# Block places in their own memory, and layer 2's residual, norm and gate as one loop over groups of three tiles

## The chip, the cores and the metric

The kernel runs on one core of a Trainium2 chip. The metric is the device time of one execution in microseconds (us). A core has five engines with an instruction stream each, which run side by side and wait for each other through semaphores: TensorE (PE; its weight loads are listed as PEld), VectorE (DVE), ScalarE (ACT), GpSimd (POOL) and SyncE (SP, which here only issues transfers). Each works through its stream in order. SBUF is the on-chip memory of 128 partitions, PSUM the banks into which TensorE writes, DRAM the memory off the core.

## What is computed

Eight layers run one after the other over 3750 nodes of 256 features and 60000 edges: four graph layers and four feed-forward layers, each added to x.

```python
x = x + L0_gnn(layernorm(x), src, dst, edge_type_8)
x = x + L0_ffn(layernorm(x))
x = x + L1_gnn(layernorm(x), edge_index)
x = x + L1_ffn(layernorm(x))
x = x + L2_gnn(layernorm(x), edge_index)
x = x + L2_ffn(layernorm(x))
x = x + L3_gnn(layernorm(x), edge_index)
x = x + L3_ffn(layernorm(x))
```

Two places matter here. Layer 0's graph part begins with a product of every node's features with the weights of 8 relations and 4 heads:

```python
feat_all = jnp.einsum('ni,rhid->rnhd', inputs, conv_weights)
feat_src_e = feat_all[edge_type, edge_src]
```

Layer 2's graph part is an attention over the incoming edges of a node. Its tail, and the gate with which the feed-forward part after it begins, are:

```python
out = agg.reshape(n, HID) + (x @ Wskip + bskip)
h = jax.nn.gelu(out, approximate=False)
y = x + h
mu = jnp.mean(y, axis=-1, keepdims=True)
var = jnp.var(y, axis=-1, keepdims=True)
return (y - mu) / jnp.sqrt(var + 1e-05) * gamma + beta
...
logits = x @ gate_w + gate_b
```

where the x of the first lines is the normalized input of the layer, and that of the last line the normalized sum after it.

## The kernel before

The 3750 nodes are NT = 30 tiles of P = 128 rows, and x (128 partitions, 30 tiles, D = 256) stays in SBUF through the whole kernel. 

**The head.** `load_edges` packs the edges, two words each, into a table `tab` in DRAM and counts in `falls` where the destinations do not rise. `l0_prepare` (L907) then runs `l0_features` (L861): it loads the weights (`l0_W`) and two attention rows (`l0_at`, one buffer, used twice), takes the statistics of all tiles, and for each tile normalizes (DVE), transposes (PE, L140, into the PSUM tile `xT_ps`), copies to `xT` (ACT, L141), forms the attention products (PE, L147, `lr_ps`, copied out by ACT at L894 and L895, the second into `l0_er`) and then four products 512 wide (`f_ps`, L147, f32). Two of the four are copied by ACT (L903) and two by DVE (L901) into `ft`, which SP stores in the table `l_feat` (L904), 1.04 MB a tile. The pools hold two `ft`, two banks each of `xT_ps` and `lr_ps`, and three of `f_ps`.

Beside this loop stand two chains on small tables, called from `beside()`. `chunks_by_dst` (L514) cuts the edges into chunks by destination: it loads `tab` into `srt` (L522), and writes tables such as `g`, `key_first`, `key_last`, `is_last` to DRAM; it opens and closes its own pools. `block_places` (L347) computes for every edge the place of its entry in a blocked adjacency matrix: it loads the table again as `bp_rec` (125 partitions, 480 edges each, L359), makes 30 counts, two small products in PSUM (`bp_ps`), and the rank loop (L396 to L401) of 30 iterations: a comparison, a scan and a predicated copy, each 125x480. It then stores `put` in `put_dram` (L423), and leaves in `over` whether an edge has found no place. A planner orders the instructions on each engine, so that the chains' instructions stand between the feature loop's. The pools of `block_places` open when those of `chunks_by_dst` are closed, and so lie in the same memory.

`irregular` (L425) adds `over` and `falls`, sums them over the partitions on PE (`falls_ps`, L432) and makes the flag (`irr_flag`, L434). The value is read into registers, and the program branches on it: a general way if it is 1, the regular one if it is 0, which is the case for this data. Nothing of what follows, layer 0's gathers (`gt<-l_feat`, L150) among it, is issued before the branch.

**Layer 2.** `l2_gnn` (L1279) makes q, skip, v and k per tile, stores skip (`sk`, the trace's `l_skip`), and runs the attention, which leaves the sums of each node in `acc` (`l_accu`). Then comes the tail, in three sweeps over the 30 tiles:

- L1338 to L1348: load the skip tile `s` (L1339, 128 KB), product with the reciprocal sum (L1341), add `s` (L1343), Gelu on ACT (L1344), normalize x (L133) and add it (L1347) into `y`, an array of 30 tiles.
- `add_normed` (L983) calls `ln_stats` (L103): statistics of all 30 tiles of y (L110, L111), one Sqrt for all.
- the loop of `add_normed`: normalize y (L133), times gamma (L992), plus beta (L993), added to x (L994), and for each tile `enter` (L1371): statistics of x (L1374, L1375), a Sqrt of one column (ACT, L1377), its reciprocal (L1378), normalize into `en_xn` (L133), store it in the token table `f_x` (L1381), two transposes (PE, L1385), a copy (ACT, L1386), the product with the gate's weights (PE, L147) and the addition of its bias into `f_lg` (DVE, L1389). The pools hold three of each of these.

When all 30 tiles of `f_lg` are there, the gate's softmax and the assignment of tokens to experts follow (L1526 and on), up to the first gather of tokens from `f_x`.

`enter` is also used by layer 3, and `load_row` loads one row and copies it to all partitions.

Of the kernel before, what the change touches and what calls it, by code (L numbers as in the profile page):

```python
# [10 lines left out]
F32 = mybir.dt.float32  # L11
BF16 = mybir.dt.bfloat16
I32 = mybir.dt.int32
# [8 lines left out]
P = 128  # L22
N = 3750
NT = 30
# [34 lines left out]
class Gnn:  # L59
# [287 lines left out]
    def block_places(self, tab):  # L347

        nc = self.nc
        self.put_dram = self.dram.tile([EP, 2, EC], I32, name="put_dram")
        with ExitStack() as st:
            pool, work, pp = self.pools(st, bpl=1, bplw=2, bplp=-1)

            def new(name, dtype=F32, n=EC):
                return pool.tile([EP, n], dtype, name="bp_" + name)
            rec = pool.tile([EP, EC, 2], I32, name="bp_rec")
            nc.sync.dma_start(flat(rec), tab[:E].rearrange("(p c) f -> p (c f)", p=EP))  # L359
            put = pool.tile([EP, 2, EC], I32, name="bp_put")  # L360
            a, b = new("a", I32), new("b", I32)
            T, S = new("T"), new("S")

            nc.vector.tensor_scalar(a, rec[:, :, 1], 7, None, op0=ALU.arith_shift_right)
            nc.vector.tensor_scalar(T, a, float(TD), None, op0=ALU.min)
            nc.vector.tensor_scalar(a, rec[:, :, 0], 10, None, op0=ALU.arith_shift_right)
            nc.vector.tensor_copy(S, a)

            nc.vector.tensor_scalar(a, rec[:, :, 0], 3, None, op0=ALU.arith_shift_right)
            nc.vector.tensor_scalar(a, a, 127, None, op0=ALU.bitwise_and)  # L370
            nc.vector.scalar_tensor_tensor(put[:, 1, :], rec[:, :, 1], 256.0, a, op0=ALU.mult, op1=ALU.add)
            same = new("same")
            nc.vector.memset(same[:, 0:1], 1.0)
            nc.vector.tensor_tensor(same[:, 1:], T[:, 1:], T[:, :EC - 1], ALU.is_equal)


            end = new("end")
            nc.vector.tensor_scalar(end, T, T[:, EC - 1:], None, op0=ALU.is_equal)
            nc.vector.scalar_tensor_tensor(end, S, 1.0, end, op0=ALU.add, op1=ALU.mult)
            cnt = new("cnt", n=NT)  # L380
            for t in range(NT):
                junk = work.tile([EP, EC], F32, name="bp_eq")
                nc.vector.tensor_scalar(junk, end, float(t + 1), None, op0=ALU.is_equal, op1=ALU.add,
                                        accum_out=cnt[:, t:t + 1])
            diag = new("diag", n=EP)
            nc.vector.tensor_scalar(diag, self.ident[:EP, :EP], T[:, 0:1], None, op0=ALU.mult)
            ps = pp.tile([EP, EP + NT], F32, name="bp_ps")
            nc.tensor.matmul(ps[:, :EP], self.ones[:EP, :EP], diag, start=True, stop=True)
            nc.vector.tensor_scalar(diag, ps[:, :EP], T[:, EC - 1:], None, op0=ALU.is_equal)
            nc.vector.tensor_tensor(diag, diag, self.before[:EP, :EP], ALU.mult)  # L390
            nc.tensor.matmul(ps[:, EP:], diag, cnt, start=True, stop=True)
            carry = new("carry", n=NT)
            nc.vector.tensor_copy(carry, ps[:, EP:])
            rank = new("rank")
            nc.vector.memset(rank, 0.0)
            for t in range(NT):  # L396
                eq = work.tile([EP, EC], F32, name="bp_eq")
                run = work.tile([EP, EC], F32, name="bp_run")
                nc.vector.tensor_scalar(eq, S, float(t), None, op0=ALU.is_equal)
                nc.vector.tensor_tensor_scan(run, same, eq, carry[:, t:t + 1], ALU.mult, ALU.add)  # L400
                nc.vector.copy_predicated(rank, eq.bitcast(I32), run)  # L401
            nc.vector.tensor_scalar(rank, rank, -1.0, None, op0=ALU.add)

            lim = end
            nc.vector.tensor_scalar(lim, T, 1.0, 256.0, op0=ALU.is_lt, op1=ALU.mult)
            small = new("small")
            nc.vector.tensor_scalar(small, T, 4.0, 128.0, op0=ALU.is_lt, op1=ALU.mult)
            nc.vector.scalar_tensor_tensor(lim, small, 128.0, lim, op0=ALU.add, op1=ALU.add)
            nc.vector.tensor_scalar(small, T, float(TD), 128.0 * (JS - 1), op0=ALU.is_ge, op1=ALU.mult)
            nc.vector.tensor_tensor(lim, lim, small, ALU.add)  # L410
            nc.vector.tensor_tensor(lim, rank, lim, ALU.is_ge)
            nc.vector.tensor_reduce(carry[:, 0:1], lim, AX.X, ALU.add)
            nc.vector.tensor_tensor(self.over, self.over, carry[:, 0:1], ALU.add)

            for t, before in ((1, T), (1, small), (1, small), (2, small), (3, small), (4, small)):
                nc.vector.scalar_tensor_tensor(small, T, float(t), before, op0=ALU.is_ge, op1=ALU.add)
            nc.vector.tensor_copy(a, rank)
            nc.vector.tensor_scalar(b, a, 7, None, op0=ALU.arith_shift_right)
            nc.vector.tensor_scalar(a, a, 127, None, op0=ALU.bitwise_and)
            nc.vector.tensor_tensor(small, small, b, ALU.add)  # L420
            nc.vector.scalar_tensor_tensor(small, small, float(NT), S, op0=ALU.mult, op1=ALU.add)
            nc.vector.scalar_tensor_tensor(put[:, 0, :], a, float(NCB), small, op0=ALU.mult, op1=ALU.add)
            nc.sync.dma_start(self.put_dram, put)  # L423
# [437 lines left out]
    def l0_features(self, tab, er, beside):  # L861
# [5 lines left out]
        with ExitStack() as st:  # L867
# [18 lines left out]
            for t in range(NT):  # L886
# [3 lines left out]
                self.transposed(xT, xn, pp)  # L890
                ft = xp.tile([P, R, D + H], F32, name="ft")
                ps = pp.tile([P, 2 * RH], F32, name="lr_ps")
# [14 lines left out]
    def l0_prepare(self, tab):  # L907

        nc, R, H = self.nc, 8, 4
        self.feat = self.dram.tile([NP * R, D + H], F32, name="l0_feat")  # L910
        self.er_dram = self.dram.tile([P, NT * R * H], F32, name="l0_er_dram")
        with ExitStack() as st:
            pool, = self.pools(st, l0er=1)
            er = pool.tile([P, NT, R * H], F32, name="l0_er")
            def beside():
                self.over = self.edges.tile([EP, 1], F32, name="over")
                self.chunks_by_dst(tab, CAPS)
                self.block_places(tab)
            self.l0_features(self.feat, er, beside)
            nc.sync.dma_start(self.er_dram, flat(er))  # L920
# [358 lines left out]
    def l2_gnn(self, entry):  # L1279
# [4 lines left out]
        with ExitStack() as outer:  # L1284
# [46 lines left out]
            with ExitStack() as st:  # L1331
                wp, ap = self.pools(st, l2fin=3, l2y=1)
# [3 lines left out]
                y = ap.tile([P, NT, D], F32, name="l2_y")  # L1336
                for t in range(NT):
                    s = wp.tile([P, D], F32, name="s")  # L1338
                    nc.sync.dma_start(s, sk[t * P:(t + 1) * P])  # L1339
                    a = wp.tile([P, H, DH], F32, name="a")  # L1340
                    nc.vector.tensor_tensor(a, acc[:, t, :D].rearrange("p (h d) -> p h d", h=H),  # L1341
                                            rd[:, t, :].unsqueeze(2).to_broadcast([P, H, DH]), ALU.mult)
                    nc.vector.tensor_tensor(flat(a), flat(a), s, ALU.add)  # L1343
                    nc.scalar.activation(flat(a), flat(a), AF.Gelu)  # L1344
                    xn = wp.tile([P, D], F32, name="xn")
                    self.normed(xn, self.x, stats, t)
                    nc.vector.tensor_tensor(y[:, t, :], xn, flat(a), ALU.add)  # L1347
                wp, pp = self.pools(st, l2en=3, l2enp=-3)  # L1348
                self.add_normed(ap, y, "L2_gnn_gamma", "L2_gnn_beta", "l2n",
                                lambda t: self.enter(entry, t, wp, pp))  # L1350
# [20 lines left out]
    def enter(self, e, t, wp, pp):  # L1371
        nc = self.nc
        st = wp.tile([P, 6], F32, name="en_st")
        nc.vector.bn_stats(st, self.x[:, t, :])  # L1374
        nc.vector.bn_aggr(e["mv"][:, t, :], st)  # L1375
        r = e["rstd"][:, t:t + 1]
        nc.scalar.activation(r, e["mv"][:, t, 1:2], AF.Sqrt, bias=self.eps, scale=1.0)  # L1377
        nc.vector.reciprocal(r, r)  # L1378
        xn = wp.tile([P, D], F32, name="en_xn")
        self.normed(xn, self.x, e["stats"], t)  # L1380
        nc.sync.dma_start(e["tab"][t * P:(t + 1) * P], xn)  # L1381
        xT = wp.tile([P, 2, P], F32, name="en_xT")
        bank = pp.tile([P, 3, P], F32, name="en_ps")
        for c in range(2):
            nc.tensor.transpose(bank[:, c, :], xn[:, c * P:(c + 1) * P], self.ident)  # L1385
        nc.scalar.copy(xT, bank[:, :2, :])  # L1386
# [924 lines left out]
```

## Time and profile before

Three runs took 5733.62, 5743.11 and 5742.64 us, the median 5742.64. The profile is of one execution of its own:

| | |
|---|---|
| profiled execution | 6525.78 us |
| its span, first to last instruction | 6524.0 us |
| mean granted TensorE clock | 0.798 |
| longer than the median of the runs by | 783 us (13.6%) |
| first gather of layer 0 | at 370.0 us |
| layer 2's tail, L1334 to the last f_lg | 3946.7 to 4116.9 us |
| first gather of layer 2's tokens | at 4165.2 us |

Times within the kernel are those of this execution. The page has the span in 40 equal slices; a digit is the busy share of a slice in tenths, and PEclk is the clock granted to TensorE in tenths of full speed:

```profile
PE   6826655596476665975555553798879898896885
DVE  5634433794233346435565557403532342266435
POOL 0046666676566658864444440012025444452124
PEclk9957777798677777987777775698589999998896
```

A slice is 163 us. The first two are the head: POOL has nothing to do in them. Slices 24 and 25 (the count starts at 0) hold layer 2's tail and the start of the feed-forward part: VectorE falls from 7 to 4, and the granted clock is 0.5 and 0.6.

### The profile page before, as it was taken

Reading aid. Unit: us, or ns where it says so; the run is one execution under the profiler, and the core shown is the slowest. Engines: PE = TensorE matmul, PEld = TensorE weight load, DVE = VectorE, ACT = ScalarE, POOL = GpSimd, SP = SyncE. Lnnn points to the kernel's source line nnn. Section 1 sums busy time; section 2 is a strip of 40 time slices with the busy share of each in tenths; the row PEclk is TensorE's granted clock in tenths of the full one; section 3 lists DMA queues with packets and bytes.
Section 4 is the critical chain, followed back from the end, with each engine's and each line's share of the span. In section 5 each row is a group of like instructions: output and inputs, shape, how many; then the busy total and the mean of one; then the engine's idle time right before and its main releaser. Section 6 shows DMA issues by size and latency. Waiting matters only on the chain. (4 is left out here: it accounts for less than half of the span.)

```text
span 6524.0 us, 64749 instructions
## 1 busy us (share of the span) xinstructions
PE 4544.5 (70%) x20324; PEld 3306.5 (51%) x20438; DVE 3068.4 (47%) x7333; ACT 2064.1 (32%) x4862; POOL 2921.8 (45%) x2845
## 2 busy tenths in 40 slices
PE   6826655596476665975555553798879898896885
PEld 2425554465455553634444442576545565564673
DVE  5634433794233346435565557403532342266435
ACT  1125544312455552324343442222531121110121
POOL 0046666676566658864444440012025444452124
PEclk9957777798677777987777775698589999998896
DMA  4334444202344431145555551222434554455113
GB/s 147 132 95 115 115 116 112 43 2 72 99 119 117 115 79 35 22 130 160 159 159 157 147 148 45 90 91 74 162 124 139 137 134 128 132 145 162 50 56 114
DMA packets 431195, 714.02 MB, mean 109 GB/s; under 512 B 117474, under 2 KB 308645, under 8 KB 426748
## 3 DMA queue, kind: packets, MB, share of 16 engines
q0 software_dynamic: 145168, 379.81, 23.0%
q1 hardware_dynamic: 267064, 316.47, 15.5%
q10 hardware_dynamic: 18612, 13.50, 0.7%
q8 instruction: 166, 2.72, 0.2%
q14 instruction: 185, 1.52, 0.1%
HBM read 583.81 MB, written 125.15 MB: 109 GB/s over the span
## 5 line engine op out<-in xcount | busy, mean ns | idle before, releaser
L1965 PE MATMUL sum_ps<-gt,oh 128*128 128x260 f32 (+2 forms) x3150 | 1018.8, 485 | 368.2 <-issue 155.4
L1965 PEld LDWEIGHTS sum_ps<-gt,oh 128*128 128x128 f32 x3150 | 749.4, 244 | 565.0 <-issue 187.7
L150 POOL DMA_INDIRECT gt<-l_vk,srci x525 | 497.6, 948 | 549.1 <-issue 179.4
L156 POOL DMA_INDIRECT blocks<-put x480 | 648.2, 1350 | 155.0 <-issue 145.6
L150 POOL DMA_INDIRECT gt<-l_h,srci x525 | 496.6, 946 | 333.8 <-issue 228.8
L150 POOL DMA_INDIRECT gt<-l_feat,g x525 | 501.7, 956 | 317.2 <-issue 235.2
L1947 DVE TENSOR_TENSOR gt<-gt,bank 128x1792 f32<-128x1792 f32 x225 | 453.5, 2016 | 123.6 <-remote 52.8
L1839 ACT ACTIVATE oh<-iota,dloc 128x128 f32<-128x128 f32 x1575 | 481.4, 386 | 19.1 <-PE sum_ps L1965 15.7
L150 POOL DMA_INDIRECT gt<-l_mtab,l_idxm x300 | 296.3, 988 | 359.9 <-ACT gt L2170 184.3
L150 POOL DMA_INDIRECT gt<-l_xtab,srci x262 | 253.2, 966 | 396.7 <-DMA l_xtab<-xt 192.4
L2184 PE MATMUL two_ps<-l_twox,slab 128*128 128x512 bf16 x1026 | 354.8, 391 | 28.1 <-issue 27.8
L147 PE MATMUL y_ps<-f_w,hT 128*128 128x256 f32 x1600 | 359.4, 384 | 15.5 <-DVE y L1075 13.5
L2184 PEld LDWEIGHTS <-slab 128*128 128x128 bf16 x2160 | 213.5, 99 | 268.2 <-issue 40.9
L2184 PE MATMUL two_ps<-l_twom,slab 128*128 128x512 bf16 x1020 | 341.9, 379 | 0.0
L147 PEld LDWEIGHTS y_ps<-f_w,hT 128*128 128x128 f32 x1600 | 306.8, 193 | 67.2 <-DVE y L1075 18.0
L2186 PE MATMUL third_ps<-l_thirdx,slab 128*128 128x257 bf16 x1080 | 300.7, 280 | 31.5 <-issue 17.6
L2186 PE MATMUL third_ps<-gt,oh 128*128 128x257 f32 x1124 | 275.4, 389 | 37.1 <-DVE oh L2173 28.5
L2186 PE MATMUL third_ps<-l_thirdm,slab 128*128 128x257 bf16 x1080 | 294.8, 273 | 3.2
L1830 ACT ACTIVATE ohT<-rows,iota_p 128x896 f32<-128x896 bf16 x225 | 235.2, 1045 | 142.8 <-DMA rows<-dl_dram 69.7
L1322 PE MATMUL q_ps<-l_qt,ohT 128*128 128x256 f32 x1050 | 250.1, 391 | 31.4 <-DVE gt L1328 18.7
L1976 PE MATMUL bank<-less,at_row 112*128 112x8 f32 (+1 forms) x146 | 41.7, 358 | 317.2 <-issue 156.9
L1922 ACT ACTIVATE fw<-fw 112x128 f32<-112x128 f32 x76 | 23.5, 309 | 754.5 <-DVE fw L1921 608.9
(544 smaller groups left out, 8807.8 us busy)
## 6 DMA issues: line engine op xcount, KB each, us to landing
rows<-dl_dram SPq DMA_DIRECT2D x225, 224.0 KB
slab<-adT SPq DMA_DIRECT2D x36, 960.0 KB
slab<-ad SPq DMA_DIRECT2D x30, 1152.0 KB
l_feat<-ft SPq DMA_DIRECT2D x30, 1040.0 KB
f_w<-in_L_ffn_w_dram SPq DMA_DIRECT2D x18, 1024.0 KB
adT<-db_rowT SPq DMA_DIRECT2D x36, 480.0 KB
ad<-db_row SPq DMA_DIRECT2D x36, 480.0 KB
f_yt<-y SPq DMA_DIRECT2D x114, 128.0 KB
```

The source lines that it names most:

```text
L147: self.nc.tensor.matmul(ps, xT[:, c, :], w[:, c, :], start=(c == 0), stop=(c == kc - 1))
L150: return self.nc.gpsimd.indirect_dma_start(out=out, out_offset=None, in_=table, in_offset=bass.IndirectOffsetOnAxis(ap=idx, axis=0))
L156: inst = self.nc.gpsimd.indirect_dma_start(out=table, out_offset=bass.IndirectOffsetOnAxis(ap=idx, axis=0), in_=src, in_offset=None)
L1322: nc.tensor.matmul(ps[:, j, :], ohT[:, j * P:(j + 1) * P], flat(q[:, ds(tiles[j], 1), :]), start=True, stop=True)
L1830: nc.scalar.activation(t, rows, AF.Abs, bias=self.iota_p, scale=-1.0)
L1839: nc.scalar.activation(oh[:, j, :], self.iota, AF.Abs, bias=self.dloc[:, c + j:c + j + 1], scale=-1.0)
L1922: nc.scalar.activation(fw, fw, AF.Exp)
L1947: nc.vector.tensor_tensor(rows, rows, wj.unsqueeze(3).to_broadcast([P, GC, H, DH]), ALU.mult)
L1965: nc.tensor.matmul(open_[1], oh[:, j, :], gt[:, j, :W], start=starts(k), stop=starts(k + 1))
L1976: nc.tensor.matmul(f_ps, at, less, start=True, stop=True)
L2184: nc.tensor.matmul(flat(ps), block, flat(two[n][:, blocks[i][1]]), start=(i == 0), stop=(i == len(blocks) - 1))
L2186: nc.tensor.matmul(ps3[:, :D + 1], block, rhs, start=(i == 0), stop=(i == len(all3) - 1))
```

## The change

In the head, `beside()` opens the pools of `block_places` before it calls `chunks_by_dst`, and hands them over, so that they no longer share memory with the chunk tables. The pool of `bp_ps`, a PSUM bank, is thereby open through both chains. The feature loop puts its transposed tile and its attention products in one tile `l0_bank` of one bank in place of two (`xT_ps` and `lr_ps`). The body of `block_places` is unindented and otherwise unchanged.

In layer 2, the tail becomes one loop over groups of T = 3 tiles in four stages: `arm` of group k, `norm` of group k-1, `join` of group k, `enter_rows` of group k-1. The skip load is one transfer of three tiles, the additions of skip, of the gated row and of beta are 768 wide, the Gelu too. The normalized x is made on ACT, as Identity with a scale and a bias. Gamma is a factor of the same operation that subtracts the mean, and the reciprocal deviation is applied with the addition to x, to which beta has been added before. The Sqrt takes three columns. The array y of 30 tiles is gone; its groups live in a pool with two buffers, as do the tiles of `enter_rows`, which had three.

```diff
-    def block_places(self, tab):
+    def block_places(self, tab, pool, work, pp):
...
-        with ExitStack() as st:
-            pool, work, pp = self.pools(st, bpl=1, bplw=2, bplp=-1)
...
-                self.transposed(xT, xn, pp)
+                bank = pp.tile([P, 2 * P + 2 * RH], F32, name="l0_bank")
+                turned, ps = bank[:, :2 * P].rearrange("p (c n) -> p c n", c=2), bank[:, 2 * P:]
+                for c in range(2):
+                    nc.tensor.transpose(turned[:, c, :], xn[:, c * P:(c + 1) * P], self.ident)
+                nc.scalar.copy(xT, turned)
                 ft = xp.tile([P, R, D + H], F32, name="ft")
-                ps = pp.tile([P, 2 * RH], F32, name="lr_ps")
                 self.product(ps, xT, wl)
...
-                self.chunks_by_dst(tab, CAPS)
-                self.block_places(tab)
+                with ExitStack() as st2:
+
+                    pools = self.pools(st2, bpl=1, bplw=2, bplp=-1)
+                    self.chunks_by_dst(tab, CAPS)
+                    self.block_places(tab, *pools)
...
-                wp, ap = self.pools(st, l2fin=3, l2y=1)
+                T = 3
+                ap, wp, pp = self.pools(st, l2y=1, l2fin=2, l2enp=-3)
                 rd = ap.tile([P, NT, H], F32, name="l2_rd")
                 nc.vector.tensor_scalar(rd, acc[:, :NT, D:], TINY, None, op0=ALU.max)
                 nc.vector.reciprocal(rd, rd)
-                y = ap.tile([P, NT, D], F32, name="l2_y")
-                for t in range(NT):
-                    s = wp.tile([P, D], F32, name="s")
-                    nc.sync.dma_start(s, sk[t * P:(t + 1) * P])
-                    a = wp.tile([P, H, DH], F32, name="a")
-                    nc.vector.tensor_tensor(a, acc[:, t, :D].rearrange("p (h d) -> p h d", h=H),
-                                            rd[:, t, :].unsqueeze(2).to_broadcast([P, H, DH]), ALU.mult)
-                    nc.vector.tensor_tensor(flat(a), flat(a), s, ALU.add)
-                    nc.scalar.activation(flat(a), flat(a), AF.Gelu)
-                    xn = wp.tile([P, D], F32, name="xn")
-                    self.normed(xn, self.x, stats, t)
-                    nc.vector.tensor_tensor(y[:, t, :], xn, flat(a), ALU.add)
-                wp, pp = self.pools(st, l2en=3, l2enp=-3)
-                self.add_normed(ap, y, "L2_gnn_gamma", "L2_gnn_beta", "l2n",
-                                lambda t: self.enter(entry, t, wp, pp))
+                gamma = self.load_row(ap, ins["L2_gnn_gamma"], "l2n_g")
+                beta = self.load_row(ap, ins["L2_gnn_beta"], "l2n_b")
+                mv, rstd = stats
+                off = ap.tile([P, NT], F32, name="l2_off")
+                nc.vector.scalar_tensor_tensor(off, mv[:, :, 0], -1.0, rstd, op0=ALU.mult, op1=ALU.mult)
+                ymv, yr = ap.tile([P, NT, 2], F32, name="l2_ymv"), ap.tile([P, NT], F32, name="l2_yr")
+                ys, arms = {}, {}
+                def arm(t0):
+                    s = wp.tile([P, T, D], F32, name="s")
+                    nc.sync.dma_start(s, sk[t0 * P:(t0 + T) * P].rearrange("(t p) d -> p t d", p=P))
+                    a = wp.tile([P, T, D], F32, name="a")
+                    for t in range(T):
+                        nc.vector.tensor_tensor(a[:, t].rearrange("p (h d) -> p h d", h=H),
+                                                acc[:, t0 + t, :D].rearrange("p (h d) -> p h d", h=H),
+                                                rd[:, t0 + t, :].unsqueeze(2).to_broadcast([P, H, DH]), ALU.mult)
+                    nc.vector.tensor_tensor(a, a, s, ALU.add)
+                    nc.scalar.activation(flat(a), flat(a), AF.Gelu)
+                    y = wp.tile([P, T, D], F32, name="y")
+                    for t in range(t0, t0 + T):
+                        nc.scalar.activation(y[:, t - t0], self.x[:, t], AF.Identity, bias=off[:, t:t + 1],
+                                             scale=rstd[:, t:t + 1])
+                    arms[t0], ys[t0] = a, y
+                def join(t0):
+                    y, x = ys[t0], self.x[:, t0:t0 + T]
+                    nc.vector.tensor_tensor(y, y, arms.pop(t0), ALU.add)
+                    for t in range(T):
+                        bn = wp.tile([P, 6], F32, name="bn")
+                        nc.vector.bn_stats(bn, y[:, t])
+                        nc.vector.bn_aggr(ymv[:, t0 + t], bn)
+                    nc.scalar.activation(yr[:, t0:t0 + T], ymv[:, t0:t0 + T, 1], AF.Sqrt, bias=self.eps, scale=1.0)
+                    nc.vector.tensor_tensor(x, x, beta.unsqueeze(1).to_broadcast([P, T, D]), ALU.add)
+                def norm(t0):
+                    y = ys.pop(t0)
+                    nc.vector.reciprocal(yr[:, t0:t0 + T], yr[:, t0:t0 + T])
+                    for t in range(t0, t0 + T):
+                        row, x = y[:, t - t0], self.x[:, t]
+                        nc.vector.scalar_tensor_tensor(row, row, ymv[:, t, 0:1], gamma, op0=ALU.subtract, op1=ALU.mult)
+                        nc.vector.scalar_tensor_tensor(x, row, yr[:, t:t + 1], x, op0=ALU.mult, op1=ALU.add)
+                    self.enter_stats(entry, t0, t0 + T, wp)
+                for t0 in range(0, NT + T, T):
+                    if t0 < NT:
+                        arm(t0)
+                    if t0:
+                        norm(t0 - T)
+                    if t0 < NT:
+                        join(t0)
+                    if t0:
+                        self.enter_rows(entry, t0 - T, t0, wp, pp)
```

`enter` is split in two. `enter_stats` holds the statistics of tiles t0 to t1 and one Sqrt over their columns; `enter_rows` holds one reciprocal over them, and for each tile the rest of `enter` unchanged: the normalized row `en_xn`, its store in `f_x`, the transposes, the copy, the product with the gate's weights and the bias. `enter` itself calls both for one tile.

## The prediction

> **What bounds the kernel now.** The page's busy row first: no engine is full, so what the change is worth must be read in its two stages.
>
> ```profile
> PE 4544.5 (70%) x20324; PEld 3306.5 (51%) x20438; DVE 3068.4 (47%) x7333; ACT 2064.1 (32%) x4862; POOL 2921.8 (45%) x2845
> ```
>
> The head next, in the timeline around the branch (start us, duration us, engine, line, operation; in brackets the idle time before and what ended it):
>
> ```profile
> 310.31 3.70 PE L147 MATMUL f_ps<-l_W,xT 128*128 128x512 f32 x8 [0.90 <-DVE ft L901]
> 318.79 0.67 DVE L901 COPY ft<-f_ps 128x512 f32<-128x512 f32 x1
> 324.11 0.72 DVE L399 TENSOR_SCALAR bp_eq<-bp_S 125x480 f32<-125x480 f32 x2
> 328.26 0.72 DVE L399 TENSOR_SCALAR bp_eq<-bp_S 125x480 f32<-125x480 f32 x2
> 350.73 0.19 PE L432 MATMUL falls_ps<-ones,over 125*1 125x1 f32 x2 [36.72 <-DVE over L430]
> 351.22 0.14 DVE L434 TENSOR_SCALAR irr_flag<-falls_ps 1x1 int32<-1x1 f32 x1
> 370.01 5.34 POOL L150 DMA_INDIRECT gt<-l_feat,g  x1 [14.23 <-DMA seg_b<-seg]
> ```
>
> TensorE ends layer 0's products at 314.0 and stands still until 350.73: VectorE works alone on the place chain, two rank iterations per 4.15 us. Only then is the flag there, on which the branch and the first gather hang. The chain is late because it starts late. In SyncE's waits (engine, line, who ended the wait: us in total, times, longest) its load stands behind the last release of the chunk tables; the tile view has that load issued at 232.6, while the table it reads was loaded once already at 46.2:
>
> ```profile
> SPq L359 <- DMA is_last_dram<-is_last: 5.6, 1, 5.6
> ```
>
> Layer 2's tail runs from 3946.66 (reciprocal) to 4116.9 (last f_lg), 170.3 us. The window rows give length, then busy us of PE, PEld, DVE, ACT, POOL with counts, the PE clock, the DMA share and GB/s; the group rows give busy us, mean ns, and the idle time before:
>
> ```profile
> 3946.50:4117.00 170.50, 50.25 (x181) 36.57 (x182) 129.62 (x466) 35.29 (x95) 0.16 (x1) 0.51 0.15 46
> 3946.50:3987.60 41.10, 0.00 (x0) 0.00 (x0) 40.67 (x118) 13.41 (x31) 0.00 (x0) 0.56 0.30 87
> L1389 DVE TENSOR_TENSOR f_lg<-en_ps,f_gb 128x8 f32<-128x8 f32 x30 | 5.0, 167 | 40.4 <-PE en_ps L147 40.4
> L1386 ACT COPY en_xT<-en_ps 128x256 f32<-128x256 f32 x30 | 11.2, 372 | 69.0 <-PE en_ps L1385 69.0
> ```
>
> VectorE sets the pace: full for 41 us, then idle 30 times for about 1.35 us (40.4 in all), each time until TensorE has one tile's gate product. TensorE, ScalarE and the transfers have room.
>
> **Part A, the head.** Removed: the wait at L359. In the changed program's order the load stands right behind the chunks' own load of that table, at about 34 us, and the chain's VectorE work lies among the 60 feature copies (L901), the last of it with 23 copies to come. No instruction is saved, so the gain is what the chain hides behind. TensorE's own pace is 15.63 us per two tiles (lr_ps at 163.03 to 178.66), 3.9 us per VectorE copy. I add the chain's rows, start to start, between the copies: a count .57, a rank iteration 2.08 ((328.26−324.11)/2), a copy .60.
> - Copies 5 to 12 carry the front of the chain: 38.4 us of VectorE from 79.19, so copy 12 at 117.6 (before 120.4).
> - Copies 13 to 19 at TensorE's pace: about 145 (before 146.7).
> - Copies 20 to 36 carry the rank loop, 80.2 us of VectorE where TensorE needs 17×3.9 = 66.3: about 225 (before 214).
> - 23 more at 3.9: about 315; the flag at 315.5 to 316 instead of 351.36. **Gain 36 us.**
>
> Before, TensorE lost 9 us here in another place:
>
> ```profile
> 114.18 1.12 PE L147 MATMUL lr_ps<-l_wlr,xT 128*128 128x64 f32 x4 [8.97 <-ACT xT L141]
> ```
>
> There a copy queued on ScalarE behind a DMA issue that waited for key_first (10.5 us). In the new order those issues (L666) stand behind the xT copies of two more tiles, so I expect 1 to 2 us of it; ScalarE's later copies and the issues queue behind it. If it stays and none of VectorE's excess (about 26 us) finds slack, the gain is 20. The upper end, 45, takes the excess as hidden.
>
> The moved load passes the second l_at load on SyncE, which is not issued before 46.2 for want of a buffer: nothing. Merging xT_ps and lr_ps in one bank makes a transpose wait for the er copy two tiles back instead of the xT copy, under 2 us after it in 7.8 us per tile: nothing. Late next are the 12 feature stores still on SyncE behind the places' store: the last, 1.04 MB at the 128 GB/s of this loop, lands 8 us after its copy, near 326; the first gather stays 18.65 us behind the flag, near 334. Were that cover gone it would cost the difference, a few us.
>
> **Part B, layer 2.** VectorE's 30 passes for the normalized input go to ScalarE, the 30 gamma products into the subtraction, the residual into the scaling; skip, gate and beta additions become 768 wide, and 31 Sqrt become 20. Rows start to start: a 256-wide operation .335 us, bn with aggregation .39, xn .325, f_lg and a reciprocal .08. A 768-wide addition is not in this stage: three times .335 is the upper end (1.0), 480 wide takes .58 and 640 wide .74, whose slope of 1.07 ns an element gives .88; I take .88. The fused operation with two inputs exists in layer 1 (L1275, L1276, 479 ns busy where a plain one shows 415), so .335 to .40; I take .335 and leave .06×60 = 4 us to the range.
>
> Per group of three: products 1.0, three wide additions (+s, +a, +beta) 2.64, six fused 2.0, six bn 2.34, xn .98, f_lg .24, reciprocals .16: 9.36 us. Ten groups 93.6, less 1.8 for two beta additions pulled into the attention's end, plus the reciprocal 1.95, plus the adjacency set-up that falls here before and after (8.4): 102.2 us, against 129.6 busy.
>
> Idle: following one period in the new order, VectorE waits about .94 us at the pair of f_lg and .64 at the third, where before it waited 1.35 per tile; 1.6 a group, nine groups 14.4 (ends 0 and 3.5 a group: 0 and 31). Tail 2 us. End 3946.7+102.2+14.4+2 = 4065: 52 us earlier, less 2 to 4 for what was pulled into the attention: **gain 48 us**, range 25 to 66. Skip loads of 393 KB go out five deep ahead, then among the f_x stores on SyncE, two groups early (22 us) at a DMA share of 0.15: hidden. ScalarE holds Gelu .9, three Identity 1.2, two Sqrt .6, three copies 1.1 and two table loads 2.6 (the other kinds' means from the stage's ACT rows, Gelu scaled up from .42 for 256, an estimate), 6.5 of 11 us. What follows hangs on f_lg (the first token gather is issued at 4165), so the whole gain passes on.
>
> **A rule against this.** Gelu and Sqrt now alternate, and each change reloads ScalarE's table: 18 loads where there were 2.
>
> ```profile
> 3987.80 0.42 ACT L1344 ACTIVATE a<-a 128x256 f32<-128x256 f32 x1 [0.91 <-DVE a L1343]
> 3988.23 1.28 ACT L112 ACT_TABLE_LOAD   x1
> ```
>
> By the row a load is 1.28 us and begins .01 after the Gelu, ahead of the Sqrt's wait; 16 more cost 20.5 us of ScalarE's 135 idle. The Trainium skill ("ScalarE: Activation LUTs", section "What ACT_TABLE_LOAD costs") adds a drain of about 1380 ns, 2.66 us a switch. The row shows none ahead of the load; what comes behind it no row of this stage shows, as ScalarE then waits for data. By the rule Gelu ends 1.4 us later, the third tile's copy waits for it, the period goes from 10.95 to 12.3 and the stage gains 36. I take the row and keep 36 in the range.
>
> **Sum.** 36+48 = 84 us of the profiled 6525.78: about 6442. The median of the plain runs is 12% shorter, so the gain lies between .88 and 1 of that; as both stages run on TensorE and VectorE without gathers, I take .95: 80 us, **5662**.
>
> **Rivals.** (1) The head becomes VectorE-bound, excess and stall staying: 20+48 = 68, 5678. For it, the rank loop needs 4.7 us a copy against 3.9; against it, the 7 copies between and slack in the six f_ps and ft buffers. Chance .15. (2) Layer 2 keeps its latencies, with drains or 3.5 to 4.5 us idle a group: 27 there, 36+27 = 63, 5683; with both short 45, 5700. For it, each f_lg waits for a chain over three engines (xn, transposes, copy, product: 2.3 to 2.6 us); against it, two tiles' chains now overlap. Chance .15, both .05. (3) Slower: the loop is serialised over ScalarE's table loads. The two stages each wait for a Gelu and a Sqrt with their loads (2.2+1.9) and two full entry chains (5) on top of 9.36: 18.5 us a period, 21.3 with drains, where it decides from 19.4 (1.95+8.4+2+10×19.4 eats the head's 36 too): at 21.3 it is 225 us, 55 longer, and with the head's 36 about 19 longer, 5761. Against it, the loads run ahead of the waits, and other stages' work stands between. Chance .04. (4) The last feature store holds the first gather anyway: it lands near 326 at most, so a few us; inside the forecast. That the places don't move is excluded by the new order.
>
> **Numbers.** The forecast .61, rivals (1) .15, (2) .15, both .05, (3) .04. The likeliest alone spans 5640 to 5680 (profiled gains 65 to 105 by the ends above); the range runs to the case of both short and some run-to-run spread (the runs of before span 9.5 us): 5632 to 5705. A difference under 0.2% (11.5 us) can't be told from none: faster .93, same .03 (the far end of both short), slower .04.
>
> **What would show it.** Flag near 316, places' load near 34, first gather near 334; TensorE's longest gap before the flag under 3 us. Layer 2's tail about 118 us, period near 11, VectorE's wait for the gate product 14 us in all, 18 loads with a Gelu or Sqrt starting right behind one. Wrong if the last product is past 330, if the gather moves less than the flag, or if periods exceed 13 us.

## The result, and the profile after

The changed kernel takes 5672.25 us (median of 4 runs, 5671.77 to 5673.43) beside 5742.51 before (4 runs): a ratio of 0.9882, 95% interval 0.9864 to 0.9899, 70 us less. The forecast was 5662 with a range of 5632 to 5705.

Its profiled execution spans 5671.6 us. The profile of before, 6524.0 us, fits a slower chip: on the chip of three of the experiments below the kernel before has a median of 6508.8 us. Which chip the profile came from is not on record. A second profile of the kernel before, on a chip where it takes 5748 us, spans 5752.2 and is used from here on for sums over the whole kernel. The head and layer 2's tail last the same in both (flag at 351.2 and 350.2, tail 170.2 us in each), so the lines shown with the prediction can be set beside the new ones.

The page of the changed kernel, busy row and VectorE's and TensorE's 40 slices of 142 us:

```profile
PE 4457.1 (79%) x20438; PEld 3256.8 (57%) x20438; DVE 3041.6 (54%) x7203; ACT 2097.9 (37%) x4877; POOL 2923.4 (52%) x2845
PE   5957777687677746988887748987799999994996
DVE  7624544895334366448888883026533433566336
```

VectorE's first slice is at 7 where it was 5, in both profiles of before: the chain has moved forward. The head's timeline, as before with start and length in us, engine, line and operation:

```profile
316.07 0.69 DVE L902 COPY ft<-f_ps 128x512 f32<-128x512 f32 x1 [3.24 <-PE f_ps L147]
319.35 0.19 PE L430 MATMUL falls_ps<-ones,over 125*1 125x1 f32 x2
319.45 0.69 DVE L902 COPY ft<-f_ps 128x512 f32<-128x512 f32 x1 [2.69 <-PE f_ps L147]
320.06 0.13 DVE L432 TENSOR_SCALAR irr_flag<-falls_ps 1x1 int32<-1x1 f32 x1
337.39 5.35 POOL L150 DMA_INDIRECT gt<-l_feat,g  x1 [9.23 <-DMA ends_b<-ends_dram]
```

TensorE's gap of 36.7 us before the flag's product is gone; VectorE now waits for TensorE at the end. The flag comes at 320.06 (before 351.22), the first gather at 337.39 (370.01). Layer 2's tail in its window row (length, then busy us of PE, PEld, DVE, ACT and POOL):

```profile
3277.50:3402.25 124.75, 46.56 (x180) 36.97 (x181) 106.48 (x331) 60.83 (x102) 0.15 (x1) 0.52 0.19 60
```

and VectorE's main wait in it (us in all, times, longest):

```profile
DVE f_lg L1440 <- PE en_ps L147: 18.1, 28, 1.3
```

The tail takes 124.75 us instead of 170. VectorE is busy 23 us less and waits 22 us less for the gate product (40.4 before).

From the second profile of before to the changed kernel's (5752.2 to 5671.6) the 80.6 us sum up so. The first gather comes 31.4 us earlier. From it to the start of the tail it is 5.3 less; two other profiles with the old head, the merged bank's and the changed tail's, are 8.3 and 6.5 us shorter there than the second profile of before, so this is put down to scatter. From the start of the tail to the first token gather it is 42.1 less (218.5 to 176.4), and the rest is 1.8.

### The profile page after: what moved, and what is told of

The parts are those of the page before. It is cut to its first block, busy times and chain, and to the rows that moved or that the text cites. A ratio compares the mean times of both kernels' runs of the same rounds, so it can differ in the third digit from the quotient of the medians.

```text
span 5671.6 us, 64613 instructions
## 1 busy us (share of the span) xinstructions
PE 4457.1 (79%) x20438; PEld 3256.8 (57%) x20438; DVE 3041.6 (54%) x7203; ACT 2097.9 (37%) x4877; POOL 2923.4 (52%) x2845
## 4 chain that ended last, share of the span: by engine, by line
PE 45%; DVE 16%; POOL 12%; DMA 9%; issue 8%; ACT 4%; DVEq 0%; SPq 0%; ACTq 0%; another core or an unknown queue 0%; POOLq 0%
POOL gt L150 11%; PE sum_ps L2016 7%; PE third_ps L2237 7%; PE two_ps L2235 5%; PE y_ps L147 5%; PE hT_ps L1824 3%; PE y_ps L1833 2%; PE h_ps L1617 2%; PE db_psT L2149 2%; PE q_ps L1326 2%; DMA gt<-l_h,srci 2%; DMA gt<-l_vk,srci 2%; PE qkvs_ps L147 2%; PE h_ps L1260 2%; DMA gt<-l_feat,g 2%
## 5 line engine op out<-in xcount | busy, mean ns | idle before, releaser
L2016 PE MATMUL sum_ps<-gt,oh 128*128 128x260 f32 (+2 forms) x3150 | 996.7, 482 | 272.3 <-ACT gt L1999 171.0
L2235 PE MATMUL two_ps<-l_twom,slab 128*128 128x512 bf16 x1080 | 359.8, 379 | 0.0
L2149 PE MATMUL db_psT<-db_oh,db_oh 128*128 128x128 bf16 x690 | 187.7, 409 | 66.9 <-ACT db_rowT L2150 32.4
L1892 ACT ACTIVATE oh<-oh,ones 128x896 f32<-128x896 f32 x225 | 234.4, 1042 | 7.3
```

The costliest lines, as they stand in the source:

```text
L1892: nc.scalar.activation(flat(oh), flat(oh), AF.Relu, bias=self.ones[:, 0:1], scale=-1.0)
L2016: nc.tensor.matmul(open_[1], oh[:, j, :], gt[:, j, :W], start=starts(k), stop=starts(k + 1))
L2149: nc.tensor.matmul(ps[:, j, :], lhsT, rhs, start=(i == 0), stop=(i == len(some) - 1))
L2235: nc.tensor.matmul(flat(ps), block, flat(two[n][:, blocks[i][1]]), start=(i == 0), stop=(i == len(blocks) - 1))
```

## The experiments

Experiments 1 to 4, 5 to 8, 9 to 11 and 12 each ran on a chip of their own, together with the kernel before.

**1. A second profile of the kernel before**

> The kernel before, unchanged, for a second profile. The first profiled execution took 6525.78 us, 783 us more than the median of the plain runs. If that execution was a single odd one, this profile spans about 5740 us, with the flag of the head near 351 us, the first gather near 370 us and layer 2's tail again about 170 us long. If the profiler always slows this kernel so, the span is again near 6520 us, and the durations in the head and in the tail can't be set beside those of the changed kernel without a scale.

5754.0 us beside 5747.7: the head and the tail as in the first profile. The 783 us lay neither in these stages nor with the profiler. The two profiles differ in the stages between: from the first gather of layer 0 to its reciprocal it is 855 us in the first and 696 here.

**2 and 3. The two halves alone.** The diffs are the two parts of the change.

> Only the head changed (pools of the block places opened early, one bank for transposed tile and attention products); layer 2's tail as before. By the traces the first gather came 32.6 us earlier (370.0 to 337.4). If everything behind the gather just shifts, this gains 30 to 33 us: about 5710. If a part is given back behind the branch (the gathers of layer 0 then start while stores are still landing), the gain is under 27 us: over 5715.

> Only layer 2's tail changed; head as before. By the traces the tail is 44.5 us shorter (170.3 to 125.8). If all of it passes on to the token gather and nothing of it depends on the head, the gain is 42 to 45 us: about 5699, and with the head's alone the two sum to the whole change (70 us). If the attention before it pays for the y passes that were pulled into its end, the gain is 38 us or less.

The head alone takes 5716.19 us (ratio 0.9946, 0.9933 to 0.9960), 31.5 less; the tail alone 5702.95 (0.9927, 0.9914 to 0.9941), 44.8 less. The sum, 76, is that of the whole change on another chip of the same kind (5752.41 to 5676.14) and, within the intervals, of the first result. The head's gain passes through undiminished, and the attention doesn't pay for the pulled-in passes beyond what these intervals show.

**4. The merged bank alone**

```diff
-                self.transposed(xT, xn, pp)
-                ps = pp.tile([P, 2 * RH], F32, name="lr_ps")
+                bank = pp.tile([P, 2 * P + 2 * RH], F32, name="l0_bank")
+                turned, ps = bank[:, :2 * P].rearrange("p (c n) -> p c n", c=2), bank[:, 2 * P:]
```

> The kernel before with only the merge of transposed tile and attention products in one PSUM bank; places and tail as before. Prediction's step: it costs nothing, within 2 us of before (5740 to 5745). Rival: a tile's transpose now waits for the second copy out of the shared bank and TensorE loses up to 0.5 us in each of 30 tiles, hidden until the end of the products behind the place chain here, so that the time is the same but TensorE's last product of the head comes up to 15 us later than 314.0.

Ratio 1.0002 (0.9994 to 1.0010), and TensorE's last product ends at 313.9 (314.0 and 313.0 in the two profiles of before): it costs nothing, and hides nothing.

**5 to 8, the changed kernel again and three edits of it**

> The changed kernel itself, on the chip of the next three, as what they are set beside: about 0.988 of before, flag of the head near 320, layer 2's tail near 125 us.

5676.14 us, ratio 0.9869 (0.9853 to 0.9886).

*One load of the table.*

```diff
-        rec = pool.tile([EP, EC, 2], I32, name="bp_rec")
-        nc.sync.dma_start(flat(rec), tab[:E].rearrange("(p c) f -> p (c f)", p=EP))
...
+                    rec = pools[0].tile([EP, EC, 2], I32, name="srt")
+                    self.nc.sync.dma_start(flat(rec), tab[:E].rearrange("(p c) f -> p (c f)", p=EP))
-                    self.chunks_by_dst(tab, CAPS)
-                    self.block_places(tab, *pools)
+                    self.chunks_by_dst(tab, CAPS, rec)
+                    self.block_places(rec, *pools)
```

> The changed kernel, but the block places use the table copy that the chunks have loaded (one tile for both), so the second load of 480 KB at 33.6 us is gone. In the changed kernel VectorE's product L879 waited 4.75 us for a weight load that ended 1.02 us of waiting before, and every later step of the head stands 3.1 us later. Theory: the second table load takes its bandwidth among the weight loads, so that product starts near 43.9 instead of 47.0, the flag comes 2 to 4 us earlier (316 to 318), the time is 2 to 4 us below the changed kernel's. Rival: the weights' lateness has another cause (the order of the loads), the product starts at 47 again and nothing is gained.

The product among the weights, first in the changed kernel's second run, then here, in VectorE's timeline:

```profile
46.78 2.29 DVE L879 TENSOR_TENSOR l_pr<-l_W,l_at 128x2048 f32<-128x2048 f32 x1 [4.87 <-DMA l_W<-_L_gnn_conv_weights_dram]
```

```profile
44.11 2.29 DVE L878 TENSOR_TENSOR l_pr<-l_W,l_at 128x2048 f32<-128x2048 f32 x1 [0.22 <-DVE l_st L110]
```

The wait for a weight load is gone. The first feature copy is at 59.85 (62.52 in the changed kernel on this chip; 59.64 and 58.64 before), the last at 316.57 against 318.59, so 2.0 us of the 2.7 reach the end of the head. The time, 5672.89, is 3 us lower, which fits but is within the intervals; the trace carries the theory.

*Key loads issued by GpSimd.*

```diff
-                    eng = (nc.sync, nc.scalar)[(i // B + c) % 2]
+                    eng = (nc.sync, nc.gpsimd)[(i // B + c) % 2]
```

> The changed kernel, but those half of the key loads (endk) that ScalarE issued are issued by GpSimd; the order on TensorE and VectorE is the same. In the changed kernel ScalarE waits 9.8 us for key_first at 121.5 and TensorE then 4.9 us for its copies. Theory: that wait goes, TensorE's 4.9 us with it, and the flag comes 4 to 5 us earlier (315 to 316). Rival: VectorE bounds this stretch by the chain's work before and behind it, and the flag moves under 1.5 us; or GpSimd issues the small loads so slowly that VectorE waits for the ends, and the flag comes later than 320.

The first run of the changed kernel, its ScalarE and then its TensorE, at that place:

```profile
122.12 0.18 ACT L895 COPY ft<-l_bank 128x32 f32<-128x32 f32 x1 [9.79 <-DMA endk<-key_first]
```

```profile
126.20 3.78 PE L147 MATMUL f_ps<-l_W,xT 128*128 128x512 f32 x4 [4.88 <-ACT ft L904]
```

A copy is ready to go and waits behind an issue that waits for its data; TensorE then waits for the buffer that the copy would free. With the issues on GpSimd:

```profile
123.32 3.65 PE L147 MATMUL f_ps<-l_W,xT 128*128 128x512 f32 x8
128.18 3.27 PE L147 MATMUL f_ps<-l_W,xT 128*128 128x512 f32 x7 [1.21 <-DVE ft L902]
```

The last copy comes at 313.91 in place of 318.59, the flag at 314.52, the gather at 332.16. The time is 5673.35 us, again within the intervals. The instruction order on TensorE and VectorE in the head is the changed kernel's own.

*No change of table.*

```diff
-                    nc.scalar.activation(flat(a), flat(a), AF.Gelu)
+                    nc.scalar.activation(flat(a), flat(a), AF.Identity)
```

> The changed kernel with layer 2's gated row as Identity in place of Gelu (this leaves out layer 2's Gelu), which needs no other table than the Sqrt: the 17 or so loads between Gelu and Sqrt in the tail go, everything else stays. Theory (the switch costs 1.28 us and lies in ScalarE's idle time): period 11.4 to 11.7 us as in the changed kernel (11.63) and the tail within 3 us of 124.8. Rival (loads and what follows them are on the path): period 10.5 or less, tail under 115 us.

The time is 5678.59 us. The 17 loads are gone, ScalarE's busy time in the tail falls from 60.8 to 39.3 us, and the tail is 128.9 us, 4 longer: the planner, which counts the loads, put the rows elsewhere, and VectorE waits 23.5 us for the gate product. VectorE's busy time is nearly the same (105.0). So taking the loads away did not shorten the tail, which speaks against the rival; what the identical order would take without them was not shown.

**9 to 11, on the slower chip (before: 6508.8 us)**

*The normalized input on VectorE again.*

```diff
-                        nc.scalar.activation(y[:, t - t0], self.x[:, t], AF.Identity, bias=off[:, t:t + 1],
-                                             scale=rstd[:, t:t + 1])
+                        nc.vector.tensor_scalar(y[:, t - t0], self.x[:, t], mv[:, t, 0:1], rstd[:, t:t + 1],
+                                                op0=ALU.subtract, op1=ALU.mult)
```

> The changed kernel with one part of the tail undone: the normalized input made by VectorE again (30 operations of .335 us from start to start) and not by ScalarE. Theory (VectorE's own work sets the period, the rest is waits for the gate product): period about 12.6 us against 11.63, tail about 133 to 135 us against 124.8. Rival (the chain over TensorE and ScalarE sets it and VectorE's work fills idle time): tail under 128 us.

Window row of the tail, then VectorE's wait:

```profile
3900.40:4034.90 134.50, 46.53 (x180) 36.93 (x181) 114.28 (x355) 48.40 (x78) 0.16 (x1) 0.52 0.18 56
DVE f_lg L1440 <- PE en_ps L147: 20.1, 30, 1.3
```

The tail takes 134.5 us with a period of 12.67 (f_lg at 3957.50, 3970.17); VectorE is busy 7.8 us more and waits 2.0 more. Its work sets the period, as the theory says. The time is 6455.74 us, ratio 0.9920 (0.9901 to 0.9939).

*Groups of 5* (`T = 5`).

> The changed kernel with groups of 5 tiles in layer 2's tail (6 groups in place of 10, 12 table loads fewer or so). In the changed kernel VectorE waits 1.70 us in a period of three tiles. Theory (one pair and the last tile of a group wait, whatever its size): about 2 to 2.5 us idle in a period of five tiles, 11 us in all against 18.1, VectorE's work the same or 2 us less, more filling at the start; tail 118 to 123 us. Rival (each gate product waits in its turn, idle goes by tile): 17 us or more idle, tail 124 us or more.

Window row of the tail, then its wait:

```profile
3921.30:4046.10 124.80, 45.34 (x180) 36.86 (x181) 105.00 (x311) 44.90 (x78) 0.15 (x1) 0.51 0.18 56
```

```profile
DVE f_lg L1440 <- PE en_ps L147: 18.9, 22, 1.4
```

The theory fell and the rival held: with 6 groups in place of 10 VectorE still waits 18.9 us. So the wait does not go with the number of groups. It belongs to the gate products, which the planner orders in pairs and single tiles; what each pair costs was not tried apart. The time is 6433.67 us, ratio 0.9878 (0.9858 to 0.9899).

*Both edits of the head.*

> The changed kernel with one load of the table for both chains, and the key loads issued by GpSimd in place of ScalarE. The first brought the flag from 319.2 to 317.2, the second to 314.5 on the same chip. If the two are independent the flag is at 311 to 313 and the first gather near 328 to 330; the time is 6 to 9 us below the changed kernel's, 0.9855 of before or less. If VectorE's chain takes the place of the wait, the flag stays at 314 or later.

The last copy comes at 309.97, the flag at 310.58, the first gather at 327.44. The two edits add up at least: apart they gave 2.0 and 4.7 us at the last copy, together 9.0 and 9.7 against the two other runs of this chip (318.93 and 319.64). Six profiles of the changed head have that copy between 318.6 and 320.2, so a us or two of it is scatter. The time is 6381.61 us; the ratio, 0.9816 (0.9784 to 0.9847), is better than the head explains. In the profiles the stretch from layer 1's reciprocal to layer 2's tail took 1465 us, against 1513 and 1530 in the other two runs of this chip and 1514 in the first profile of before; why wasn't settled, and it stays open.

**12. Both edits of the head, and groups of 2** (`T = 2`)

> The head of the last run but one (one load of the table, key loads issued by GpSimd) and groups of 2 tiles in layer 2's tail, where the planner puts the table load of the Exp behind the tail ahead of the cast that it stood behind. Head: flag at 310 to 313 again, first gather 327 to 330. Tail, if the wait goes by tile as the groups of 5 showed (19 us there, 18 of 3): 16 to 20 us idle again, VectorE's work 2 to 4 us more than 106.5 for the shorter additions, tail 126 to 130. If it goes by pairs that end a group, 15 waits in place of 20, the idle is under 14 and the tail at or under 124. Exp: from the last gate product to the row maximum behind it 1.5 to 2 us as before the change, in place of 5.5. In all within 3 us of the run with groups of 3, and 6 to 12 us below the changed kernel.

5663.19 us, ratio 0.9852 (0.9835 to 0.9868) on a chip where before takes 5745.88: 83 us under before. Each of its runs (5654.62 to 5665.98) lies below each of the changed kernel's (5671.73 to 5683.92), but those did not run beside it, and the intervals of the ratios overlap: that it beats the changed kernel too is likely, not shown. The flag comes at 313.26, just past the range expected. The tail's window row, then its wait:

```profile
3275.70:3395.06 119.36, 44.50 (x180) 36.95 (x180) 106.26 (x353) 79.87 (x131) 0.15 (x1) 0.52 0.21 65
```

```profile
DVE f_lg L1441 <- PE en_ps L147: 11.5, 10, 1.3
```

ScalarE is busy two thirds of the time, with 28 table loads, and VectorE waits only 11.5 us: the alternative in the expectation, idle by pairs, was right. Three of the four adjacency operations (`db_oh`, 1.2 us each; one of them in the changed kernel) now lie behind the tail, so the row maximum after the Exp is the fairer end to compare: it starts 123.9 us after the tail's start, in the changed kernel 130.1, in the second profile of before 171.5. Of the 4.5 us between the last gate product and that row maximum those operations hold 3.5; the Exp itself no longer waits for its table. Not all of the 6.2 us gained on the changed kernel passes on: the first token gather comes 172.1 us after the tail's start, against 176.4.

## Why the prediction was right, and where its sum was off

Direction and mechanism hold for both halves: the flag no longer waits for the chain, and the tail is VectorE's work plus a smaller wait. The gain was put at 84 us of the profile; from trace to trace it is about 74 (31.4 at the first gather, 42.1 at the token gather).

**Head, 36 predicted, 31.4 found.** The last copy was put at 315 and came at 319.45. By the terms of the sum:
- The moved load, "nothing": 3.1 us. Only its place in SyncE's queue was looked at, and that was right; its 480 KB travel among the weight loads, and a weight came later by that much. Without it, in the run with one load, the product among the weights came 2.7 earlier (46.78 to 44.11).
- Copies 5 to 12, 38.4 us: 39.7.
- ScalarE's queued issue, "1 to 2 us": 4.9 us of TensorE, and copies 13 to 19 took 31.8 in place of 27.3. Moving the issues behind two xT copies only made another copy the victim. With them on GpSimd the last copy came 4.7 earlier on the same chip. The sign "TensorE's longest gap under 3 us" failed here.
- The rank loop, 80.2 us: 79.6 (153.77 to 233.40). The bound was right: start-to-start sums of rows of the one engine, taken where it is full.
- The last 23 copies, 89.7: 86.1.

The merged bank costs nothing, as the fourth run shows, and the last store held up nothing: the gather follows the flag by 17.3 us, before by 18.8, and its wait ends with the load of `ends_b`. The rival with a VectorE-bound head was half right: the ScalarE wait stayed, but the rest of the loop had the slack for VectorE's excess.

**Tail, 118.6 predicted, 124.75 found.** VectorE's work 106.5 in place of 102.2: the fused operations go every .395 us and not .335, 60 × .06 = 3.6 us, which the text left to the range (the 768-wide additions went every .84, not .88). The wait is 18.1 in place of 14.4, and the period 11.63 in place of 10.95. That VectorE's work sets it, the ninth run confirms (12.67 for a forecast of 12.6). What the fused passes, the wide additions and the single loop are worth each was not run apart, and that the wait fell from 40.4 us because the chains of two tiles overlap is read from the order of the rows, not tested.

**The table loads.** ScalarE in one period:

```profile
3327.70 0.80 ACT L1438 COPY en_xT<-en_ps 128x256 f32<-128x256 f32 x2 [0.86 <-PE en_ps L1437]
3328.51 1.28 ACT L1359 ACT_TABLE_LOAD   x1
3329.81 0.84 ACT L1359 ACTIVATE a<-a 128x768 f32<-128x768 f32 x1
```

The load starts .01 us after the copies and the Gelu .02 after the load: the whole switch costs 1.30 us. The drain of about 1380 ns that the Trainium skill adds ("ScalarE: Activation LUTs", section "What ACT_TABLE_LOAD costs") is on neither side; the row was the right choice, and the 12 us that the rule would have cost did not come. The eighth run agrees, in another order of the rows: without the loads the tail was no shorter.

**What the whole gain was to pass on.** It didn't quite. From the end of the last gate product to the first token gather it is 51.6 us where it was 48.4. The Exp's table load and the row maximum behind the Exp, in the second profile of before:

```profile
3483.01 1.28 ACT L1528 ACT_TABLE_LOAD   x1
3485.69 0.40 DVE L1529 TENSOR_REDUCE f_mx<-f_lg 128x30 f32<-128x240 f32 x1 [0.47 <-ACT f_lg L1528]
```

and in the changed kernel, from the last gate product on:

```profile
3402.08 0.17 DVE L1440 TENSOR_TENSOR f_lg<-en_ps,f_gb 128x8 f32<-128x8 f32 x1 [1.32 <-PE en_ps L147]
3405.26 0.58 ACT L2150 CAST db_rowT<-db_psT 128x512 bf16<-128x512 f32 x1 [4.36 <-PE db_psT L2149]
3405.86 1.28 ACT L1579 ACT_TABLE_LOAD   x1
3407.59 0.40 DVE L1580 TENSOR_REDUCE f_mx<-f_lg 128x30 f32<-128x240 f32 x1 [3.19 <-ACT f_lg L1579]
```

Before, the Exp's table was loaded right after the last copy (which ends at 3482.99), ahead of the Exp's data. Now the load stands behind a cast that waits 4.36 us for TensorE, and the row maximum starts 5.3 us after the last gate product where it was 1.3. In both traces the load runs ahead of its data only as far as its place in the queue lets it, and this cost was not in the sum. It is not the only cause: in the twelfth run the load is early again, and from the last gate product to the token gather it is 52.8 us. What else delays that gather was not followed.

**The scale of .95** for the plain runs rested on a wrong reading: the first profile was longer in stages that the change doesn't touch, most likely because of its chip, and head and tail last the same in both. The scale was 1. That its 4 us made good a part of the 10 us that the sum had too much was luck; of the 80 forecast, 70 and 76 were found on two chips.

**Three slips without weight.** The table "loaded once already at 46.2" was loaded earlier: its load goes out at 33.5, and 46.2 is VectorE's first operation on it. VectorE's excess of "about 26 us" is 21 by the two stretches named (7.2 and 13.9). The gains of the two rivals, 20 and 27, add up to 47, not 45.

## What to carry to other kernels

A load that is moved is not free because its queue has room: ask which other transfers share its time, and which of them somebody waits for. An issue that waits for data holds up every copy behind it on its engine (here 9.8 us of ScalarE); put on an idle engine, it held up nothing. Before a profile's own time is scaled to the plain runs, see in which stages the two differ.

## What was not expected of the hardware

Some chips run the same program in about 5745 us and one in about 6509 (mean granted TensorE clock 0.84 and 0.80). From the first gather of layer 0 to its reciprocal, where all these kernels have the same code, it is 848 to 858 us in the three profiles of the slower chip, 855 in the first profile of before, and 693 to 696 in the other ten. The gathers' own durations are the same in both profiles of before (median 946 ns), and the head and the tail keep theirs to within about 1 us. Why the stages with gathers stretch was not found.
